# Attention masks of one key tile moved from VectorE to TensorE in a four-layer graph network, with a new written-out order of the work

## The chip, the cores and the metric

The kernel runs on one core of one Trainium2 chip. The metric is the device time of one launch in microseconds (us). TensorE (PE in the profile) multiplies matrices, VectorE (DVE) and ScalarE (ACT) work element by element, GpSimd (POOL) does a few small powers, and SyncE (SP) issues the transfers. The engines run side by side, each through its own list of instructions in order, and wait for each other by semaphores. TensorE writes to PSUM[...].

## The reference, cut to what matters

32 graphs of 512 nodes with 256 features pass through four attention layers; `adj` holds which nodes are neighbours. Layers 0, 1 and 3 are graph attention layers. Layer 2 is a transformer block whose attention has 8 heads of 32 features and is allowed only where either direction of the edge exists, or on the diagonal:

```python
allowed = (adj > 0) | (jnp.swapaxes(adj, 1, 2) > 0) | eye
scores = jnp.einsum('bhqd,bhkd->bhqk', q * scale, k)
scores = jnp.where(allowed[:, None], scores, -jnp.inf)
attn = jax.nn.softmax(scores, axis=-1)
ctx = jnp.einsum('bhqk,bhkd->bhqd', attn, v)
```

After it come an output projection, a layer norm, a feed-forward block of 1024 hidden features, and two more norms. Layers 0 and 1 precede it, layer 3 follows it, and each layer ends in a residual sum and a norm.

## The kernel before, in words

Nodes are cut into R = 4 tiles of P = 128 partitions. One graph of 32 (a batch below) is a Python generator, `graph` (L718), that runs through its stages: loads, layer 0, layer 1, the symmetric mask, qkv, attention, projection, feed forward, layer 3. Each stage is cut by `yield` into units. `paced` (L108) gives each unit a place, `PERIOD * b + PLACES[stage][i]` (L27, L28), and the 32 generators are merged by these places. So the order of the instructions is a list written out by hand, repeated for every batch with a shift of PERIOD; about three and a half batches are in flight at once. The order is fixed as merged for TensorE; the other engines' lists are laid by the framework's scheduler. The size of a place doesn't stand for time on the chip: only the order counts.

What the prediction's steps touch:

- `mask` (L353) makes `at`, the transposed adjacency in bytes, with ScalarE: a cast (L362) and a sum of squares (L370) for each half.
- `symmetric` (L373) makes `a2`: for each half of the rows, VectorE takes the maximum of `at` and a half of `adj` (L381, two rows of tiles in one instruction), then sets the diagonal with a maximum with the identity (L385). `a2` is 0 or 1 in bytes. `adj` and `adjt` halves share one buffer (`half`, L347).
- `qkv` (L483) makes queries and keys. Each is split into a high and a low fp32r part (`hi` on ScalarE L502, `lo` on VectorE L503), and 64 transfers of SyncE (L510) lay four groups of 32 rows out per head, so that one fp32r matmul of 128 rows gives a score at higher precision.
- `attention` (L533): for each of four head pairs and each of four key tiles j, two score matmuls (`s`, 512 columns, one per head) go to PSUM, ScalarE takes the exp (L549), and VectorE multiplies both heads by the mask of that key tile in one instruction of 1024 elements (L550, L551). After the four tiles of a pair come eight context matmuls (`cp`, L557 on), two for each j in the order of j, the two heads in different halves of the columns. `v` holds a column of ones, so the row sums come with them. ScalarE copies the result (`cs`, L567).
- `attended` (L571) turns the contexts by TensorE (`ctp` from `cs`), divides by the row sums on VectorE (L582, L586: `ctx`), turns them again (`ctp` from `ctx`) and projects (`wop`).
- `feed_forward` (L610) alternates `f1p` on TensorE, relu on ScalarE (`ft`, L633) and `f2p`.
- `layernorm` (L259) takes statistics on VectorE (L265, L266, L268), a power of -1/2 on GpSimd (L269), a product on VectorE (L270), and scale and bias on ScalarE (L274). `head_layernorm` (L282), in layer 0, has a power of GpSimd (L296) and then a product on VectorE (L297).
- `along` (L335) spreads a column of exps over all rows by transposes (`gp`) and a copy (`gb`, L344); VectorE makes `pt` from it (L391), and `o` is the product with it.

All matmuls of the program are issued at L101; an fp32 one is two instructions in the profile, an fp32r one and a transpose are one. PSUM is divided into two banks for each of the stages "a" and "c" and four for stage "b", to which qkv, attention and projection belong (`bank`, L247).

In steady state TensorE's list for one batch's length is this (unit and number of the program's matmuls; `ctpv` is `ctp` from `ctx`, `o0` is layer 0's `o`, `o1` layer 1's or 3's; units of several batches lie side by side):

```
s4 f2p4 s2 f1p4 s2 f2p4 cp8 s4 f1p4 s4 f2p4 cp8 xt1p4 f1p4 xt1p4 s4 f2p4
s2 h1p2 f1p4 h1p2 s2 h1p4 f2p4 gp4 cp8 s2 f1p4 s4 f2p4 o1:4 s2 o1:4 cp8
o1:4 ctp4 o1:4 ctp8 h0p2 ctp4 h0p2 ctpv8 xt3p4 h0p4 xt3p4 wop2 h3p2 gp4 h3p6
wop2 gp4 xt2p4 wop2 xt2p4 o0:16 wop2 gp4 o1:4 qkp6 o1:12 o0:16 gp4 ytp4 qkp2
ytp4 vp4 o0:8 f1p4 o0:8 gp4 f2p4 f1p4 o0:8 f2p4 o0:8 f1p4 vp4
```

Of the kernel before, what the change touches and what calls it, by code (L numbers as in the profile page):

```python
# [20 lines left out]


F32R = mybir.dt.float32r


PERIOD = 1205
PLACES = {  # L27
    "edges": [-226, -113, -5, -1],  # L28
    "x": [84],
    "mask": [1464, 1488, 1689, 1689],  # L30
    "layer 0": [
        188, 232, 373, 373, 427, 532, 536, 536, 536, 549, 603, 603, 603, 630, 637, 712, 712, 728,
        758, 758, 766, 779, 787, 791,
    ],
    "layer 1": [1024, 1057, 1078, 1123, 1135, 1135, 1151, 1276, 1299, 1366, 1385],
    "qkv": [1656, 1721, 1771, 1771, 1771, 1849, 1893, 1903, 2016, 2028],
    "attention": [
        1976, 2013, 2122, 2148, 2174, 2174, 2174, 2178, 2178, 2217, 2277, 2277, 2278, 2333, 2363,
        2405, 2452, 2475, 2493, 2527,
    ],  # L40
    "projection": [2590, 2597, 2597, 2606, 2687, 2722, 2820, 2876, 2902, 2949],
    "feed forward": [
        3051, 3062, 3135, 3169, 3169, 3196, 3221, 3327, 3328, 3357, 3381, 3419, 3447, 3483, 3512,
        3560, 3618, 3683,
    ],
    "layer 3": [3958, 3998, 4038, 4074, 4074, 4074, 4082, 4179, 4182, 4185, 4185],
}
STAGES = {"edges": "a", "x": "a", "layer 0": "a", "layer 1": "a", "feed forward": "c", "layer 3": "c"}
ALL = mybir.DependencyInfo(mybir.DependencyClass.Sync, mybir.DependencyReason.DATA)
# [22 lines left out]
def fast_path(ctx: ExitStack, tc: tile.TileContext, a: dict, out: bass.AP, bad: bass.AP):  # L72
# [8 lines left out]
    nc = tc.nc  # L81
    B, N, D = a["x"].shape
    P = 128
    R = N // P
# [15 lines left out]
    def product(what, *args, **kwargs):  # L100
        latest[0] = what(*args, **kwargs).ins.name  # L101

    def in_place(op):

        if latest[0]:
            tc.add_manual_dep(op.ins, latest[0], ALL, reason="in its place")

    def paced(b, name, units):  # L108

        i = 0  # L110
        while True:
            stage[0] = STAGES.get(name, "b")
            try:
# [9 lines left out]
    identb = const.tile([P, P], BF16, name="identb")  # L123
# [115 lines left out]
    sb = ctx.enter_context(tc.tile_pool(name="sb", bufs=1))  # L239
# [107 lines left out]
    def half(b, name, h):  # L347
        t = sb.tile([P, R // 2, N], I32, tag="adj", name=name, bufs=1)
        rows = a[name][b, h * N // 2 : (h + 1) * N // 2]
        nc.sync.dma_start(t, rows.rearrange("(r p) j -> p r j", p=P))  # L350
        return t

    def mask(b):  # L353

        at = sb.tile([P, R, N], U8, tag="at", name="at", bufs=4)
        for h in range(2):
            yield
            t = half(b, "adjt", h)
# [12 lines left out]
        return at  # L371

    def symmetric(b, at):  # L373

        a2 = sb.tile([P, R, N], U8, tag="a2", name="a2", bufs=1)
        for h in range(2):
            yield
            t = half(b, "adj", h)
            rows = slice(h * R // 2, (h + 1) * R // 2)
            yield  # L380
            in_place(nc.vector.tensor_max(a2[:, rows, :], at[:, rows, :], t))  # L381
            for r in range(R // 2):
                own = h * R // 2 + r
                diag = a2[:, own, own * P : (own + 1) * P]
                nc.vector.tensor_max(diag, diag, identb)  # L385
        return a2

    def kept(name, g, edges, f):

# [93 lines left out]
    def qkv(x):  # L483
        xt = yield from transposed([x[:, r, :] for r in range(R)], "xt2")
        qk = []
        for c in range(K):
            t = [sb.tile([P, 2, 2, N], F32R, tag="qk", name="qk", bufs=3) for _ in range(2)]
            for s in range(2):
# [41 lines left out]

        return qk

    def attention(qk, a2):  # L533
        cs = []
        for hp in range(H2 // 2):
            pr = []
            for j in range(R):
                yield
                t = sb.tile([P, 2, N], F32, tag="pr", name="pr", bufs=4)
                for i in range(2):  # L540
                    s = bank("s")
                    product(nc.tensor.matmul,
                    s,
                        qk[hp][:, 1, i, j * P : (j + 1) * P],
                        qk[hp][:, 0, i, :],
                        start=True,
                        stop=True,
                    )
                    nc.scalar.activation(t[:, i, :], s, AF.Exp, scale=QSCALE)  # L549
                edges = a2[:, j, :].unsqueeze(1).to_broadcast([P, 2, N])  # L550
                nc.vector.tensor_mul(t, t, edges)  # L551
                pr.append(t)

            yield
            cp = bank("cp")
            for j in range(R):
                for i in range(2):  # L557
                    first = (2 * hp + i) * VC
                    product(nc.tensor.matmul,
                    cp[i * 2 * DH : (i + 1) * 2 * DH, :],  # L560
                        v[:, j, first : first + 2 * DH],
                        pr[j][:, i, :],
                        start=j == 0,
                        stop=j == R - 1,
                    )
            t = part("cs")
            nc.scalar.copy(t, cp)  # L567
            cs.append(t)
        return cs
# [106 lines left out]
    def load_x(b):  # L676
        xt = sb.tile([P, K, N], F32, tag="xt0", name="xt0", bufs=1)
        nc.sync.dma_start(xt, a["xt"][b].rearrange("(k p) n -> p k n", p=P))
        if b == 0:
            weights0()  # L680
        yield
        x = sb.tile([P, R, D], F32, tag="x", name="x")
        nc.sync.dma_start(x, a["x"][b].rearrange("(r p) d -> p r d", p=P))
        return xt, x

    def layer0_all(b, x, xt, at, rd):
        if b == 0:
# [30 lines left out]
    def graph(b):  # L718
        yield PERIOD * b + PLACES["edges"][0]
        rd = sb.tile([P, ND], F32, tag="rd", name="rd", bufs=3)  # L720
        rds = [rd[:, ends[i] : ends[i + 1]] for i in range(4)]
        if b == 0:
            xt, x = yield from paced(b, "x", load_x(b))
        at = yield from paced(b, "edges", mask(b))
        if b:
            xt, x = yield from paced(b, "x", load_x(b))
        x = yield from paced(b, "layer 0", layer0_all(b, x, xt, at, rds[0]))
        x = yield from paced(b, "layer 1", layer1_all(b, x, at, rds[1]))
        a2 = yield from paced(b, "mask", symmetric(b, at))
        qk = yield from paced(b, "qkv", qkv_all(b, x))  # L730
        cs = yield from paced(b, "attention", attention(qk, a2))
        y = yield from paced(b, "projection", attended_all(b, x, cs, rds[2]))
        x = yield from paced(b, "feed forward", feed_forward_all(b, x, y))
        x = yield from paced(b, "layer 3", layer3_all(b, x, at, rds[3]))
        nc.sync.dma_start(out[b].rearrange("(r p) d -> p r d", p=P), x)
        nc.vector.scalar_tensor_tensor(ok, rd, RD_MIN, ok, op0=ALU.is_ge, op1=ALU.mult)
        nc.vector.scalar_tensor_tensor(ok, rd, RD_MAX, ok, op0=ALU.is_le, op1=ALU.mult)
# [658 lines left out]
```

## Time and profile before

| | |
|---|---|
| runs of the kernel | 3955.46, 3956.56, 3960.7 us; median 3956.56 |
| profiled execution | 3958.95 us, of which the span from first to last instruction is 3957.2 |
| mean granted TensorE clock | 0.973 |
| TensorE, VectorE, ScalarE, GpSimd busy | 3722.2, 2830.4, 1947.7, 362.0 us |
| masking of the probabilities (L551) | 512 instructions, 1216 ns each, 616.7 us busy |
| exp of the scores (L549) | 1024 instructions, 615 ns each |
| scores (`s`) | 1024 matmuls, context (`cp`) 2048 |
| maxima of the mask (L381) | 64 instructions, 1220 ns each |

The profile is of one execution. It gives busy time by engine; the groups of instructions by line; waits, each put down to what ended last; the timeline of each engine; and busy time by windows. In a timeline a line such as "2043.37 2.80 PE L101 MATMUL cp<-pr,v ... x12" says that twelve matmuls that write `cp` from `pr` and `v` began at 2043.37 us and took 2.80 together; what stands in brackets is the time that the engine was idle before, and what ended it. "L101" is the helper's line. The ends of matmuls are modelled and overlap the next one's start, so distances are better taken from start to start.

### The profile page before, as it was taken

How to read it: one execution, taken by the hardware profiler on the slowest of the kernel's cores; microseconds unless marked ns; L12 is line 12 of the kernel's file. 1: busy time of each engine (PE TensorE's matmuls, PEld its weight loads, DVE VectorE, ACT ScalarE, POOL GpSimd, SP SyncE). 2: the span in 40 equal slices, each digit the busy share in tenths (PEclk: the TensorE clock that was granted, in tenths of full speed). 3: DMA queues.
4: the chain of work that ended last, by engine and by line, in shares of the span. 5: the costliest groups of instructions: out<-in, count | busy, mean ns of one | idle time of the engine just before them, and what ended most of it. 6: DMA issues, size and time to landing. Idle time of an engine off the chain costs nothing.

```text
span 3957.2 us, 53344 instructions
## 1 busy us (share of the span) xinstructions
PE 3722.2 (94%) x18982; PEld 2832.6 (72%) x18982; DVE 2830.4 (72%) x5626; ACT 1947.7 (49%) x4257; POOL 362.0 (9%) x266
## 2 busy tenths in 40 slices
PE   5899999999999999999999999999999999999996
PEld 4577777777777777777777777777777777777665
DVE  4667777777777777777777777777777777777753
ACT  2444455544455544455554455544455554555442
POOL 0000010010010101010101010101011101011000
PEclk6899999999999999999999999999999999999998
DMA  3222212222222222222222222222222222221110
GB/s 105 75 72 67 70 58 63 70 75 69 68 58 63 70 75 69 68 61 61 69 75 75 62 64 63 64 75 75 62 64 63 65 79 71 62 67 55 52 50 12
DMA packets 180433, 261.20 MB, mean 66 GB/s; under 512 B 36801, under 2 KB 72769, under 8 KB 180161
## 3 DMA queue, kind: packets, MB, share of 16 engines
q1 hardware_dynamic: 180160, 257.71, 23.0%
q8 instruction: 154, 2.52, 0.3%
q14 instruction: 119, 0.97, 0.1%
HBM read 106.57 MB, written 16.78 MB: 31 GB/s over the span
## 4 chain that ended last, share of the span: by engine, by line
PE 51%; DVE 17%; issue 10%; ACT 7%; POOL 7%; SPq 2%; DMA 1%; DVEq 0%; POOLq 0%; ACTq 0%
PE o L101 12%; PE f1p L101 7%; PE f2p L101 6%; DVE pr L551 5%; PE cp L101 4%; POOL rs L269 4%; PE qkp L101 3%; PE h3p L101 3%; POOL st L296 3%; PE wop L101 3%; PE h1p L101 3%; ACT y L274 2%; SPq L510 2%; DVE bn L265 2%; ACT pr L549 2%
## 5 line engine op out<-in xcount | busy, mean ns | idle before, releaser
L551 DVE TENSOR_TENSOR pr<-pr,a 128x1024 f32<-128x1024 f32 x512 | 616.7, 1216 | 220.4 <-ACT pr L549 220.2
L391 DVE SCALAR_TENSOR_TENSOR pt<-gb,ex,at 128x512 f32<-128x512 f32 x768 | 533.3, 743 | 136.3 <-ACT gb L344 136.3
L274 ACT ACTIVATE y<-y,rs 128x256 f32<-128x256 f32 x768 | 397.9, 589 | 386.0 <-DVE rs L270 385.9
L549 ACT ACTIVATE pr<-s 128x512 f32<-128x512 f32 x1024 | 542.3, 615 | 68.7 <-PE s L101 68.3
L101 PE MATMUL cp<-pr,v 128*64 128x512 f32 x2048 | 485.0, 605 | 64.7 <-DVE pr L551 64.7
L101 PEld LDWEIGHTS o<-hv,pt 128*128 128x128 f32 x4096 | 506.1, 198 | 32.6 <-DVE pt L391 16.0
L101 PE MATMUL o<-hv,pt 128*128 128x65 f32 x4096 | 507.2, 280 | 15.4 <-DVE pt L391 11.3
L101 PE MATMUL f2p<-wf,ft 128*128 128x256 f32 x2048 | 492.5, 383 | 23.2 <-ACT ft L633 22.9
L101 PE MATMUL f1p<-yt,wf 128*128 128x256 f32 x2048 | 488.7, 381 | 0.3 <-DVE yt L301 0.3
L101 PE MATMUL o<-h,pt 128*128 128x257 f32 x2048 | 482.5, 383 | 3.2 <-DVE pt L391 3.1
L101 PEld LDWEIGHTS o<-h,pt 128*128 128x128 f32 x2048 | 381.1, 190 | 97.0 <-ACT y L274 23.5
L101 PEld LDWEIGHTS f2p<-wf,ft 128*128 128x128 f32 x2048 | 379.1, 190 | 95.6 <-ACT ft L633 46.8
L633 ACT ACTIVATE ft<-f1p,cols 128x256 f32<-128x256 f32 x512 | 216.7, 479 | 454.5 <-PE f1p L101 454.5
L269 POOL TENSOR_TENSOR rs<-rs,mhalf 128x4 f32<-128x4 f32 x192 | 234.9, 1224 | 2146.4 <-DVE rs L268 2092.5
L101 PEld LDWEIGHTS f1p<-yt,wf 128*128 128x128 f32 x2048 | 382.4, 190 | 52.3 <-issue 0.8
L101 PEld LDWEIGHTS cp<-pr,v 128*64 128x64 f32 x2048 | 127.9, 137 | 346.0 <-DVE pr L551 150.3
L101 PE MATMUL s<-qk 128*128 128x512 f32 x1024 | 359.1, 456 | 1.8 <-ACT pr L549 1.7
L265 DVE BATCH_NORM_STATS2 bn<-y 128x6 f32<-128x256 f32 x768 | 295.8, 409 | 3.5
L101 PEld LDWEIGHTS s<-qk 128*128 128x128 f32 x1024 | 187.0, 190 | 97.9 <-issue 52.7
L101 PE MATMUL qkp<-xt,wqkv 128*128 128x512 f32 x512 | 232.2, 596 | 0.9 <-DVE xt L301 0.9
L296 POOL TENSOR_TENSOR st<-st,mhalf 128x16 f32<-128x16 f32 x32 | 120.9, 3779 | 978.3 <-DVE st L295 978.3
L567 ACT COPY cs<-cp 128x512 f32<-128x512 f32 x128 | 74.5, 582 | 259.6 <-PE cp L101 259.6
(129 smaller groups left out, 4500.0 us busy)
## 6 DMA issues: line engine op xcount, KB each, us to landing
qk<-hi SPq DMA_DIRECT2D x1024, 64.0 KB, 2.0
qk<-lo SPq DMA_DIRECT2D x1024, 64.0 KB, 2.0
adjt<-in_adjt SPq DMA_DIRECT2D x64, 512.0 KB, 3.3
adj<-in_adj SPq DMA_DIRECT2D x64, 512.0 KB, 3.4
xt<-in_xt SPq DMA_DIRECT2D x32, 512.0 KB, 3.6
x<-in_x SPq DMA_DIRECT2D x32, 512.0 KB, 3.6
out<-y SPq DMA_DIRECT2D x32, 512.0 KB, 3.1
wf<-in_w1t SPq DMA_DIRECT2D x1, 1024.0 KB, 7.9
```

Source lines behind the costliest of these rows:

```text
L101: latest[0] = what(*args, **kwargs).ins.name
L265: nc.vector.bn_stats(st[:, r, :], y[:, r, :])
L269: nc.gpsimd.tensor_tensor(rs[:, 1, :], rs[:, 0, :], mhalf[:, :R], op=ALU.pow)
L274: nc.scalar.activation(y[:, r, :], y[:, r, :], AF.Identity, bias=rs[:, 2, r : r + 1], scale=rs[:, 1, r : r + 1],)
L296: nc.gpsimd.tensor_tensor(st[:, 2, :], st[:, 1, :], mhalf[:, :G], op=ALU.pow)
L391: nc.vector.scalar_tensor_tensor(t, g, f, edges, op0=ALU.max, op1=ALU.mult)
L510: nc.sync.dma_start(t[hh // 2][g * DH : (g + 1) * DH, s, hh % 2, :].bitcast(F32), src[hh * DH : (hh + 1) * DH].bitcast(F32),)
L549: nc.scalar.activation(t[:, i, :], s, AF.Exp, scale=QSCALE)
L551: nc.vector.tensor_mul(t, t, edges)
L567: nc.scalar.copy(t, cp)
L633: nc.scalar.activation(ft[:, f, :], p[:, f, :], AF.Relu, bias=bf1[:, ff + f : ff + f + 1])
```

## The change

1. `symmetric` makes masks of tiles 0 to 2 as before, in bytes, but one row of tiles in each instruction. That of tile 3 goes into a bf16 tile `shut`, which is then turned into 0 where an edge is allowed and -2^127 where not, by one more instruction of VectorE.
2. In `attention`, for j = 3 each score gets a second matmul into the same bank, identity times `shut`, both bf16, which adds the mask to the score before the exp; the multiplication on VectorE is left out for that tile. For j = 0 to 2 nothing changes.
3. PERIOD and all of PLACES are new, in units of a tenth of the old ones.

```diff
+SHUT = -(2.0**127)
-PERIOD = 1205
+PERIOD = 12054
 PLACES = {
...
     "attention": [
-        1976, 2013, 2122, 2148, 2174, 2174, 2174, 2178, 2178, 2217, 2277, 2277, 2278, 2333, 2363,
-        2405, 2452, 2475, 2493, 2527,
+        20262, 20932, 21922, 21982, 22092, 22092, 22092, 22350, 22350, 23077, 23537, 23537,
+        24028, 24208, 24328, 24532, 25064, 25220, 25368, 25943,
     ],
...
     def symmetric(b, at):
 
-        a2 = sb.tile([P, R, N], U8, tag="a2", name="a2", bufs=1)
+        a2 = sb.tile([P, R - 1, N], U8, tag="a2", name="a2", bufs=1)
+        shut = sb.tile([P, N], BF16, tag="shut", name="shut", bufs=1)
+        parts = [a2[:, r, :] for r in range(R - 1)] + [shut]
         for h in range(2):
             yield
             t = half(b, "adj", h)
-            rows = slice(h * R // 2, (h + 1) * R // 2)
             yield
-            in_place(nc.vector.tensor_max(a2[:, rows, :], at[:, rows, :], t))
-            for r in range(R // 2):
-                own = h * R // 2 + r
-                diag = a2[:, own, own * P : (own + 1) * P]
+            for r in range(h * R // 2, (h + 1) * R // 2):
+                in_place(nc.vector.tensor_max(parts[r], at[:, r, :], t[:, r % (R // 2), :]))
+                diag = parts[r][:, r * P : (r + 1) * P]
                 nc.vector.tensor_max(diag, diag, identb)
-        return a2
+        nc.vector.tensor_scalar(shut, shut, 0.0, SHUT, op0=ALU.is_equal, op1=ALU.mult)
+        return a2, shut
...
                         start=True,
-                        stop=True,
+                        stop=j < R - 1,
                     )
+                    if j == R - 1:
+                        product(nc.tensor.matmul, s, identb, shut, start=False, stop=True)
                     nc.scalar.activation(t[:, i, :], s, AF.Exp, scale=QSCALE)
-                edges = a2[:, j, :].unsqueeze(1).to_broadcast([P, 2, N])
-                nc.vector.tensor_mul(t, t, edges)
+                if j < R - 1:
+                    edges = a2[:, j, :].unsqueeze(1).to_broadcast([P, 2, N])
+                    nc.vector.tensor_mul(t, t, edges)
```

With it TensorE's list for one batch's length becomes (`s*` is a score of j = 3 followed by its identity product; all else as above):

```
s4 f2p4 s2 f1p4 s*2 f2p4 cp8 s4 f1p4 s2 s*2 f2p4 f1p4 cp8 xt1p8 f2p4
h1p2 s4 f1p4 h1p6 s2 f2p4 gp4 s*2 cp8 s2 f1p4 s4 f2p4 o1:4 s*2 o1:4 cp8
o1:4 ctp16 o1:4 h0p2 xt3p8 ctpv4 h0p2 ctpv4 h0p4 wop2 h3p2 wop2 h3p2 gp4 wop2 h3p4
gp4 xt2p8 wop2 o0:16 gp4 o1:8 qkp6 o1:8 o0:16 gp4 ytp4 qkp2
ytp4 vp4 o0:12 f1p4 o0:4 gp4 f2p4 f1p4 o0:8 f2p4 o0:8 f1p4 vp4
```

SyncE has the same transfers in both; in the new order the two loads of `adj` no longer follow each other, the load of `xt` stands between them. On VectorE the third mask of the first head pair now stands ahead of the step that feeds GpSimd's power (L295); before, it stood between that step and the product that waits for the power (L297), and the mask of j = 3 stood behind the product. On ScalarE a pair of mask instructions (L362, L370) stands ahead of the copy `cs` of the fourth head pair.

More of the change, by code (lines that the diff above doesn't have):

```diff
@@ L23 @@
 F32R = mybir.dt.float32r
-PERIOD = 1205
+SHUT = -(2.0**127)
+PERIOD = 12054
 PLACES = {
-    "edges": [-226, -113, -5, -1],
-    "x": [84],
-    "mask": [1464, 1488, 1689, 1689],
+    "edges": [-1440, -1440, -410, 1420],
+    "x": [3260],
+    "mask": [16220, 16520, 16600, 17520],
     "layer 0": [
-        188, 232, 373, 373, 427, 532, 536, 536, 536, 549, 603, 603, 603, 630, 637, 712, 712, 728,
-        758, 758, 766, 779, 787, 791,
-    ],
-    "layer 1": [1024, 1057, 1078, 1123, 1135, 1135, 1151, 1276, 1299, 1366, 1385],
-    "qkv": [1656, 1721, 1771, 1771, 1771, 1849, 1893, 1903, 2016, 2028],
+        2410, 3594, 4534, 4534, 5073, 5753, 5753, 5823, 6123, 6123, 6233, 6233, 6603, 6773, 6903,
+        7687, 7687, 7777, 8077, 8077, 8157, 8287, 8439, 8439,
+    ],
+    "layer 1": [11037, 11066, 11277, 11729, 11849, 11879, 12043, 13286, 13554, 14195, 14884],
+    "qkv": [17180, 17740, 18270, 18270, 18270, 18990, 19484, 19654, 21635, 21635],
     "attention": [
-        1976, 2013, 2122, 2148, 2174, 2174, 2174, 2178, 2178, 2217, 2277, 2277, 2278, 2333, 2363,
-        2405, 2452, 2475, 2493, 2527,
+        20262, 20932, 21922, 21982, 22092, 22092, 22092, 22350, 22350, 23077, 23537, 23537,
+        24028, 24208, 24328, 24532, 25064, 25220, 25368, 25943,
     ],
-    "projection": [2590, 2597, 2597, 2606, 2687, 2722, 2820, 2876, 2902, 2949],
+    "projection": [26801, 26801, 26861, 26911, 27661, 27721, 28721, 29140, 29256, 29848],
     "feed forward": [
-        3051, 3062, 3135, 3169, 3169, 3196, 3221, 3327, 3328, 3357, 3381, 3419, 3447, 3483, 3512,
-        3560, 3618, 3683,
+        31013, 31120, 32042, 32263, 32263, 32465, 32710, 33771, 33983, 34076, 34284, 34691,
+        35070, 35329, 35615, 36103, 36646, 37299,
     ],
-    "layer 3": [3958, 3998, 4038, 4074, 4074, 4074, 4082, 4179, 4182, 4185, 4185],
+    "layer 3": [39714, 39714, 40906, 41226, 41406, 41526, 41526, 42359, 42359, 42379, 42379],
 }
@@ L531, in qkv, with attention @@
         return qk
-    def attention(qk, a2):
+    def attention(qk, a2, shut):
         cs = []
@@ L730, in graph @@
         qk = yield from paced(b, "qkv", qkv_all(b, x))
-        cs = yield from paced(b, "attention", attention(qk, a2))
+        cs = yield from paced(b, "attention", attention(qk, *a2))
         y = yield from paced(b, "projection", attended_all(b, x, cs, rds[2]))
```

## Prediction

> **What bounds the kernel now.** I read the page's first two parts first.
>
> ```profile
> PE 3722.2 (94%) x18982; PEld 2832.6 (72%) x18982; DVE 2830.4 (72%) x5626; ACT 1947.7 (49%) x4257; POOL 362.0 (9%) x266
> ...
> PEclk6899999999999999999999999999999999999998
> ```
>
> TensorE (PE) is busy 94%; nothing else is close. The time is therefore TensorE's work plus what TensorE waits. Waits by waiting engine, TensorE's own, show who keeps it (us in total, times, longest):
>
> ```profile
> PE cp L101 <- DVE pr L551: 64.7, 65, 1.9
> PE ctp L101 <- DVE ctx L586: 51.3, 61, 1.7
> PE f2p L101 <- ACT ft L633: 22.9, 39, 3.2
> ```
>
> 65 waits in 32 batches is two a batch for masked probabilities, and two for the contexts. Ends of matmuls are modelled, so these totals are too small; I take stalls from start to start in the timeline of TensorE (start, us, ..., number of instructions; one fp32 matmul of the program is two).
>
> ```profile
> 1967.61 3.65 PE L101 MATMUL cp<-pr,v 128*64 128x512 f32 x16
> 1971.19 2.00 PE L101 MATMUL o<-h,pt 128*128 128x257 f32 x8
> ...
> 2040.13 0.82 PE L101 MATMUL s<-qk 128*128 128x512 f32 x2
> 2041.44 1.99 PE L101 MATMUL f2p<-wf,ft 128*128 128x256 f32 x8 [0.49 <-ACT ft L633]
> 2043.37 2.80 PE L101 MATMUL cp<-pr,v 128*64 128x512 f32 x12
> 2047.01 1.08 PE L101 MATMUL cp<-pr,v 128*64 128x512 f32 x4 [0.84 <-DVE pr L551]
> 2048.01 1.28 PE L101 MATMUL s<-qk 128*128 128x512 f32 x4
> ...
> 2053.60 2.79 PE L101 MATMUL cp<-pr,v 128*64 128x512 f32 x12
> 2057.51 1.08 PE L101 MATMUL cp<-pr,v 128*64 128x512 f32 x4 [1.11 <-DVE pr L551]
> 2058.52 0.65 PE L101 MATMUL xt1p<-ident,y 128*128 128x128 f32 x4
> ```
>
> An unhindered context group takes 3.58 us (1967.61 to 1971.19). The first head pair's takes 4.64, the second's 4.92: stalls of 1.06 and 1.34, each in front of the last four matmuls, key tile j=3. Pairs three and four have none. The feed-forward product behind the first pair's last scores starts 1.31 after those began, where the pair before them was followed after 0.66 (2037.94 to 2038.60): 0.65 lost. VectorE's timeline tells why the first mask is late: it stands behind a normalization that waits for GpSimd.
>
> ```profile
> 2044.59 1.22 DVE L297 TENSOR_TENSOR y<-y,st 128x1024 f32<-128x1024 f32 x1 [2.79 <-POOL st L296]
> 2045.73 1.22 DVE L551 TENSOR_TENSOR pr<-pr,a 128x1024 f32<-128x1024 f32 x1
> ```
>
> The third stall, once a batch, in TensorE's timeline, and then in the busy time by windows (length; busy PE, PEld, DVE, ACT, POOL; clock; DMA):
>
> ```profile
> 2095.60 0.38 PE L101 MATMUL ctp<-ident,ctx 128*128 128x128 f32 x2
> 2096.24 0.33 PE L101 MATMUL ctp<-ident,ctx 128*128 128x128 f32 x1 [0.26 <-DVE ctx L586]
> 2098.01 1.16 PE L101 MATMUL ctp<-ident,ctx 128*128 128x128 f32 x5 [1.44 <-DVE ctx L586]
> ```
>
> ```profile
> 2095.00:2098.20 3.20, 1.50 (x9) 0.92 (x8) 3.15 (x12) 2.61 (x6) 0.00 (x0) 1.00 0.00 0
> 2098.20:2102.00 3.80, 3.80 (x15) 3.35 (x15) 2.34 (x6) 2.52 (x5) 1.01 (x1) 0.55 0.28 105
> ```
>
> Eight transposes take 0.87; in another batch they run from 1978.39 to 1981.40, so 2.14 is stall. After it the clock falls to about half in many batches: on the chain the GpSimd powers of L296 follow each other by 118.9 us (7 of 10 batches) or 117.2 (3), 118.43 on average. The halved clock costs 1.2 a batch.
>
> [...] No bf16 matmul is in this trace; the nearest row is the one-pass fp32r score, also 512 columns. Eight f1p and four scores take 2.65 (2049.13 to 2051.78); less 8 x 0.216 this leaves 0.23 a score[...]. [...] here fp32 loads of 190 hide under 216 to 230. [...] Here 1.50 busy of 3.20 was enough[...]: a half-idle window may do it. [...]
>
> **The change, part by part**, per batch in steady state. Orders are from both kernels' instruction lists, which hold no times.
>
> *Identity products.* Eight bf16 matmuls of 512 columns on TensorE, the bound. Each 0.23 (the score's step[...]): +1.84. [...] High end: if the load of ident doesn't hide, 0.23 + 0.19 = 0.42, +3.4. [...]
>
> *Masks that go.* Four L551 a batch, 4 x 1.22 = 4.9 on VectorE; the two maxima of 1.22 become four of 0.69, and one small bf16 tensor_scalar, some 0.3, is added: VectorE net -4.2. It isn't the bound, so this is worth only the stalls. Tile j=3 now needs scores and exp alone, which end 2.6 or more before its context matmuls want them (three pairs of tiles run first). First pair: stall gone, -1.06; its j=0 to 2 masks stand ahead of the GpSimd wait, as before. Second pair: -1.34 for j=3. But the third mask now stands ahead of L295 (GpSimd starts 1.2 later), a `lo` of 0.74 stands in the same chain, and the bo addition (1.2) ahead of the second pair's j=2; against this the j=3 mask (1.2) behind the normalization is gone. So VectorE is 1.4 to 2 later there while TensorE is about 1 earlier; an f1p group (1.73) moved ahead of the contexts covers most. I count it from row durations: j=2 is masked 0.5 after it is wanted: +0.5.
>
> *Feed-forward product.* The two identity products put 0.46 of cover between f1p and f2p: 0.65 becomes 0.2, -0.45.
>
> *Contexts.* All sixteen head transposes now stand together, then o (1.73), h0p (0.9), xt3p x8 (0.87), and only then the context transposes. VectorE needs four times 0.6: covered, -2.14, and -1.2 for the clock if no half-idle window is left. What is late next is xt3p, ahead of them, which wants layer 2's second norm. In the kernel before that was ready (L274, 1978.06 + 2.07) 16.55 after the last f2p (1963.58). In the new order TensorE arrives after about 14.8. The j=3 mask (1.2) is gone from the chain and the context steps stand behind it, L476 and L478 (1.3) ahead: 15.65, so +0.65. ScalarE's mask casts L362 and L370 (2.3) now stand before the copy `cs` of the fourth pair: about 0.3 late for the transposes, +0.3.
>
> *Layer 3.* The transposes for gb3 now follow h3p directly; before, wop x4 (0.87) stood between and hid the h copy (0.37), the exp (0.21) and two handovers. With that cover gone, +0.85.
>
> *Layer 0.* A third of o's four rows moves ahead of f1p, and `lo` leaves the run of pt products: the stall of 0.32 there (sixteen o from 2017.20 to 2019.28, 2.08 against 16 x 0.11) goes, -0.3.
>
> *SyncE.* The same loads; the second adj half now stands behind the xt load, which waits for h0p. It lands 3.4 us after issue and its maximum is over 8 us later: nothing; if that cover fails, the maximum and, behind it on VectorE, xt2 wait for it. Sixty-four qk copies keep their places.
>
> Sum: 1.84 + 0.5 + 0.65 + 0.3 + 0.85 - 1.06 - 1.34 - 0.45 - 2.14 - 1.2 - 0.3 = -2.35 a batch. Thirty batches run in this state (start and drain left as they are): -70. The profiled execution took 3958.95 (span 3957.2 and 1.75 around), 2.4 above the median of the runs: 3888.5 from it, 3886 from the median. I take 3887.
>
> **The rivals.**
> - *The new waits are smaller than counted.* VectorE has 28% idle and is relieved. If half of the 2.3 of new waits don't come: -3.5 a batch, 3852. For it: my counts leave no credit for waits that overlap. Against: each hangs on a named chain.
> - *The change doesn't do what it says: the stalls only move.* The norm before xt3p ends as late as now; TensorE waits there, and the clock halves as now. Then the 2.14 + 1.2 and the +0.95 against them cancel: -2.35 + 2.39 = about 0, 3958. For it: the chain before was 16.55 long, 1.8 longer than the new order allows.
> - *Slower: the change of type.* Each bf16 product stands between fp32r scores. If the loads on both sides are exposed (0.19 each, the score's own load), a product costs 0.61, not 0.23: +3.0 a batch, net +0.7, 3977. It decides from 0.23 + 2.35/8 = 0.52. Against: fp32 and fp32r follow each other now without such a cost.
>
> **How the numbers follow.** A measurement of this kernel can tell about 0.2% (8 us) from no change. Chances: the count (3866 to 3915) 0.48; smaller waits (3838 to 3866) 0.18; stalls moved, wholly or partly (3915 to 3962) 0.19, of which 0.06 is within 0.2%; type change or a like cost, slower, 0.13; faster still 0.02. Faster 0.48 + 0.18 + 0.13 + 0.02 = 0.81, same 0.06, slower 0.13. The range, 3838 to 3960, leaves out the last two and the edge of the third; it holds the high end of the products (0.19 x 8 x 30 = +46: 3933).
>
> **What would show it.** Right: no wait of cp on pr, small waits of xt3p on L274's successor and of gp on ex3, PEclk at 1.00 after the contexts, starts of score and identity product 0.23 apart, 116 us between successive powers. Wrong: identity products over 0.5 apart, or a wait of 2 us at xt3p with the clock halved behind it.

## The result, and the profile after

The changed kernel takes 3909.1 us (median of four runs, 3906.41 to 3910.59) against 3957.5 for the kernel before in the same session: a ratio of 0.9876, 95% interval 0.9862 to 0.989. The profiled execution has a span of 3904.6 us and a mean granted TensorE clock of 0.983 (before: 0.973). The gain is 48.4 us or 1.61 us a batch over thirty batches, where 70 were forecast.

GpSimd's power in layer 0's norm marks the batches. Before, its starts were 118.9 or 117.2 us apart, 118.4 on average. After (L297; line numbers of the changed kernel are one to five higher), from GpSimd's timeline:

```profile
1898.55 2.90 POOL L297 TENSOR_TENSOR st<-st,mhalf 128x16 f32<-128x16 f32 x1 [29.83 <-DVE st L296]
2015.33 2.90 POOL L297 TENSOR_TENSOR st<-st,mhalf 128x16 f32<-128x16 f32 x1 [29.83 <-DVE st L296]
```

They are 116.77 or 116.78 apart all through the steady state: 1.63 less a batch, and thirty times that is 49 us, the whole gain. The page's first part:

```profile
PE 3753.3 (96%) x19238; PEld 2824.5 (72%) x19238; DVE 2674.8 (69%) x5594; ACT 1926.2 (49%) x4257; POOL 346.9 (9%) x266
```

TensorE is busier than before (3722.2), VectorE less busy (2830.4). A mask on VectorE (L556) costs what it did, 1216 ns; there are 384 instead of 512. The maxima of 512 elements (L384), which the forecast put at 0.69 us, take 0.675 into bytes and 0.684 into `shut` (rows of 512 elements took 0.683 at L647 and 0.687 at L478 before), and the new instruction that scales `shut` (L387) takes 0.283. TensorE's waits after (us in total, times, longest):

```profile
PE xt3p L102 <- ACT y L275: 31.1, 94, 12.0
PE gp L102 <- ACT ex L665: 22.9, 32, 1.0
...
PE cp L102 <- DVE pr L556: 17.1, 30, 2.7
```

Before, `cp` on `pr` had 64.7 us and `ctp` on `ctx` 51.3. The second is gone and the first is a quarter. Two new ones have come: `gp` had 0.7, and `xt3p` 16.9 in two waits, where it now waits 94 times. In one batch of TensorE's timeline: the identity products, the contexts of the second head pair, and the two new waits.

```profile
1896.87 0.58 PE L102 MATMUL s<-qk 128*128 128x512 f32 x1
1897.30 0.39 PE L102 MATMUL s<-shut,identb 128*128 128x512 bf16 x1
...
1897.98 1.95 PE L102 MATMUL f2p<-wf,ft 128*128 128x256 f32 x8
...
1911.24 1.94 PE L102 MATMUL cp<-pr,v 128*64 128x512 f32 x8
1913.66 1.94 PE L102 MATMUL cp<-pr,v 128*64 128x512 f32 x8 [0.49 <-DVE pr L556]
1915.53 1.10 PE L102 MATMUL xt1p<-ident,y 128*128 128x128 f32 x8
...
1950.07 1.05 PE L102 MATMUL h0p<-w,xt 128*128 128x264 f32 x4
1951.12 0.33 PE L102 MATMUL xt3p<-ident,y 128*128 128x128 f32 x1
1951.61 0.33 PE L102 MATMUL xt3p<-ident,y 128*128 128x128 f32 x1 [0.16 <-ACT y L275]
...
1953.20 0.60 PE L102 MATMUL ctp<-ident,ctx 128*128 128x128 f32 x4
...
1961.56 2.01 PE L102 MATMUL h3p<-w3g,xt 128*128 128x258 f32 x8
1964.27 0.65 PE L102 MATMUL gp<-ident,ex 128*128 128x128 f32 x4 [0.70 <-ACT ex L665]
```

Two scores with their products take 1.11 (1896.87 to 1897.98); two plain scores take 0.66, so a product is 0.225. Only such sums can be read: a score's start and its product's lie 0.43 apart, the product's and the next score's 0.03, and a score with its product takes 0.46 (1896.87 to 1897.33). The sixteen `cp` of the second pair take 4.29 where 3.58 is their pace: 0.71 of stall, each end read from the next start. From the `h0p` ahead of `xt3p` to the `ctp` behind it are 3.13 us; four `h0p` take 0.89 (1953.64 to 1954.53 elsewhere) and eight transposes 0.87, so 1.37 is stall. That is more than the brackets show (0.16 each at 1951.61, 1952.10 and 1952.60), since they are counted from modelled ends. `h3p` to `gp` is 2.71 for eight products of 1.74 in all: 0.97. And the clock, busy time by windows behind that stretch (length; busy PE, PEld, DVE, ACT, POOL; clock; DMA):

```profile
1953.60:1958.00 4.40, 4.40 (x24) 3.83 (x23) 4.33 (x11) 2.38 (x7) 0.55 (x1) 1.00 0.02 6
```

The window ahead, 1949.00 to 1953.60, has TensorE 4.11 of 4.60 us busy, with the wait in short pieces; the clock granted behind it is 1.00, where in the stretch that the prediction shows it was 0.55. Over the 27 batches from the third power of layer 0 to the thirtieth, the trace's record of the granted clock has 18 spells of half clock before, of 3.41 us each, and one after, in the first of these batches. The clock in a spell is 0.5 in that record; from these numbers I estimate that a spell loses half of its length and that the spells before cost 1.1 a batch (1.2 in the forecast).

### The profile page after: what moved, and what is told of

Read it like the earlier page. It is cut to its first block, busy times and chain, and to the rows that moved or that the text cites. A ratio compares the mean times of both kernels' runs of the same rounds, so it can differ in the third digit from the quotient of the medians.

```text
span 3904.6 us, 53602 instructions
## 1 busy us (share of the span) xinstructions
PE 3753.3 (96%) x19238; PEld 2824.5 (72%) x19238; DVE 2674.8 (69%) x5594; ACT 1926.2 (49%) x4257; POOL 346.9 (9%) x266
## 3 DMA queue, kind: packets, MB, share of 16 engines
q1 hardware_dynamic: 180160, 257.71, 23.1%
## 4 chain that ended last, share of the span: by engine, by line
PE 60%; DVE 14%; issue 8%; ACT 5%; POOL 5%; POOLq 0%; ACTq 0%
PE o L102 16%; PE f1p L102 7%; PE f2p L102 6%; PE qkp L102 5%; PE cp L102 5%; DVE pr L556 4%; ACT y L275 4%; POOL rs L270 3%; PE h3p L102 3%; PE s L102 3%; PE h1p L102 3%; PE wop L102 3%; POOL st L297 2%; PE gp L102 2%; PE vp L102 2%
## 5 line engine op out<-in xcount | busy, mean ns | idle before, releaser
L556 DVE TENSOR_TENSOR pr<-pr,a 128x1024 f32<-128x1024 f32 x384 | 459.1, 1216 | 319.3 <-ACT pr L553 319.2
L102 PE MATMUL f2p<-wf,ft 128*128 128x256 f32 x2048 | 491.6, 383 | 12.3 <-ACT ft L638 12.2
L102 PE MATMUL cp<-pr,v 128*64 128x512 f32 x2048 | 474.9, 600 | 17.8 <-DVE pr L556 17.1
L270 POOL TENSOR_TENSOR rs<-rs,mhalf 128x4 f32<-128x4 f32 x192 | 246.2, 1282 | 2118.8 <-DVE rs L269 1826.0
L102 PEld LDWEIGHTS f2p<-wf,ft 128*128 128x128 f32 x2048 | 380.1, 191 | 69.5 <-ACT ft L638 17.1
L102 PE MATMUL s<-qk 128*128 128x512 f32 x1024 | 395.1, 481 | 1.6 <-ACT pr L553 1.6
L345 ACT COPY gb<-gp 128x512 f32<-128x512 f32 x192 | 111.5, 581 | 219.4 <-PE gp L102 219.4
L428 DVE RECIPROCAL rd<-o 128x4 f32<-128x4 f32 x128 | 23.4, 183 | 272.7 <-PE o L102 272.7
```

The costliest lines, as they stand in the source:

```text
L270: nc.gpsimd.tensor_tensor(rs[:, 1, :], rs[:, 0, :], mhalf[:, :R], op=ALU.pow)
L345: nc.scalar.copy(g, p)
L428: nc.vector.reciprocal(rdh, o[:, :, HO:])
```

## The experiments

The theory after the result: the forecast's mechanism holds, the masks' stalls and the contexts' stall go, and the shortfall is new waits (`xt3p`, `gp`, second pair) that were priced too low. Rivals: the new order alone does it; the identity products alone do it; the products cost more or less than 0.225; the new waits can be won back by moving two steps.

### The two halves apart

**e1: the kernel before with PERIOD and PLACES of the changed one, all masks on VectorE.**

```diff
-PERIOD = 1205
+PERIOD = 12054
 PLACES = {
...
```

> The new order with all four masks on VectorE. Theory A (the gain comes from the first two head pairs' waits that the identity products take away, and from the order of the contexts; the two need each other): TensorE saves the eight products (8 x 0.225 = 1.8 us a batch), but the mask of j = 3 comes late again in pairs one, two and three (about 1.1, 1.5 and 0.5 a batch) and f2p waits 0.45 more; net some +1.5 a batch, about 3950 us, with waits of cp on pr back at 60 us or more. Theory B (the order alone brings the gain): 3909 less 30 x 1.8, about 3855 us, cp waits below 30 us.

Measured: 3951.05 us, ratio to before 0.9979 (0.9971 to 0.9987), powers 118.2 apart: theory A's time. Its waits of TensorE:

```profile
PE cp L101 <- DVE pr L551: 79.0, 66, 3.1
PE xt3p L101 <- ACT y L274: 36.2, 93, 12.1
```

The order alone takes the contexts' stall away (no row of `ctp` on `ctx` is left) and raises the mean granted clock to 0.982 (0.973 before, 0.983 in the changed kernel), and it brings `xt3p` and `gp` (23.1); what is left of its gain is 8.5 us. The stall on `pr` it makes no smaller, 79.0 against 64.7. So of the changed kernel's waits those of `xt3p` and `gp` belong to the order, and what the identity products give is `cp`'s: 17.1 in place of 79.0.

**e2: the changed kernel with PERIOD and PLACES of the one before.**

```diff
-PERIOD = 12054
+PERIOD = 1205
 PLACES = {
...
```

> The identity products in the old order. Theory A: the waits of cp go (-2.4 us a batch), f2p's halves (-0.45), the products cost 1.8, and the stall at the contexts stays for the most part (about 1.7 of 2.14, the clock halved behind it in part of the batches): about -1.5 a batch, 3905 to 3915 us. The new waits on layer 2's second norm and on gb3 do not appear. Theory B: without the new order no gain, 3950 us or more.

Measured: 4004.84 us, ratio 1.0113 (1.0096 to 1.013). Theory A failed; the time is in theory B's range.

```profile
PE h0p L102 <- ACT exp L477: 57.1, 30, 1.9
```

The stalls at `pr` are gone as expected (8.5 us left), and the stall of the contexts with them (5.4). In their place `h0p` waits for its bank until ScalarE's exp of layer 1 has read it, 1.9 us a batch, and `h3p` for its input (32.6). ScalarE's timeline, of the kernel before and then of e2, tells why that exp is late:

```profile
1976.88 0.47 ACT L475 ACTIVATE exp<-o,rd 128x256 f32<-128x256 f32 x1
1978.06 2.07 ACT L274 ACTIVATE y<-y,rs 128x256 f32<-128x256 f32 x4 [0.71 <-DVE rs L270]
```

```profile
2001.32 2.07 ACT L275 ACTIVATE y<-y,rs 128x256 f32<-128x256 f32 x4 [0.73 <-DVE rs L271]
...
2003.65 0.45 ACT L477 ACTIVATE exp<-o,rd 128x256 f32<-128x256 f32 x1
```

Layer 1's last exp stood ahead of layer 2's norm and stands behind it in e2. `h3p`'s input comes from a copy on VectorE that now stands behind the sum of L400 (2009.55, the copy 2010.68) and stood ahead of it (1985.17 and 1984.26). TensorE's order is that of before; the framework has laid the lists of the two other engines anew, as in e3 and e4 below. So e2 changes more than the masks, and what the identity products would be worth in the old order with those lists as they were stays open. As measured, neither half is worth the whole: -8.5 us for the order, +45 for the masks, -48 for both.

### The price of the identity products

**e3: each identity product twice, with half the constant, so that the sum is the same.**

```diff
-SHUT = -(2.0**127)
+SHUT = -(2.0**126)
...
+                        product(nc.tensor.matmul, s, identb, shut, start=False, stop=False)
                         product(nc.tensor.matmul, s, identb, shut, start=False, stop=True)
```

> As the changed kernel, with each identity product made twice and the mask halved (2^126), so that the sum is the same. It measures the price of one product on the path: at 0.225 us each 8 x 0.225 = 1.8 a batch, of which the waits at xt3p and before the second pair's contexts may take in up to 0.8: 1.0 to 1.8 a batch, 3939 to 3963 us. If a product between two types cost 0.4 or more, 4005 us or more.

Measured: 4109.62 us, ratio 1.038 (1.0363 to 1.0397). 256 products of 0.225 are 58 us; this is 200 more than the changed kernel takes, in the range that I had given to a dear product. One wait tells where it is from, and it isn't the products': `f2p` on `ft` (L639) has 114.3 us, 38 times, up to 3.8, where the changed kernel has 12.2. The scheduler that lays ScalarE's list had put layer 0's norm ahead of the two relus that `f2p` wants. So the price can't be read here; e11 and e12 below do it.

**e11: without the identity products of head pairs one and two. e12: without all of them.** Nothing takes their place: the fourth key tile is left unmasked there, so part of the computation is missing.

```diff
-                        stop=j < R - 1,
+                        stop=j < R - 1 or hp < 2,
...
-                    if j == R - 1:
+                    if j == R - 1 and hp > 1:
```

> The changed kernel without the identity products of the first two pairs of heads; nothing takes their place, so there the fourth key tile is left without its mask (that part of the computation is left out). The lists of ScalarE and VectorE are those of the changed kernel but for two instructions, so the products' price can be read: 128 of them at 0.225 us are 28.8 us of TensorE. If TensorE's time is what counts where they stand, 3880-3886 us. If they lie where TensorE waits anyway (pair two's wait for pr, 0.7 us a batch, grows by what they leave), 3885-3900 us. If a change of type inside an accumulation costs 0.6 us instead of 0.23 beyond what the trace shows, 3830-3845 us.

> The same with all 256 identity products left out, the fourth tile unmasked in all pairs (left out). 57.6 us of TensorE at 0.225 us each. If all of it is on the path, 3850-3856 us; if xt3p and gp, whose steps on ScalarE don't come earlier, take back part of it as longer waits, 3856-3885 us; no change of the time if the products were covered.

Measured: e11 3903.63 us (ratio 0.9867, 0.9852 to 0.9883), e12 3884.91 us (0.9816, 0.9803 to 0.9829). e11 lies above all three ranges of its expectation, e12 at the upper end of its second. Of 28.8 us of TensorE in pairs one and two 5.5 come out, less than the 6 us by which the interval reaches to either side; in the steady state nothing does, the powers are 116.8 apart in both. The time comes back as waits: in e11 `cp` on `pr` has 28.7 us (17.1 in the changed kernel) and `f2p` on `ft` comes 38 times (11). From start to start, `f2p` follows the first pair's last two scores after 1.07 (1894.61 to 1895.68; 1.11 with the products), and the second pair's sixteen `cp` take 4.77 (1908.50 to 1913.27; 4.29). So 0.41 and 0.48 of the four products' 0.90 come back there. VectorE's timeline tells what sets that: the reciprocal behind layer 0's last sums, and the third mask of the second pair. In the changed kernel, and then in e11:

```profile
1888.64 0.18 DVE L428 RECIPROCAL rd<-o 128x4 f32<-128x4 f32 x1 [5.34 <-PE o L102]
...
1912.39 1.22 DVE L556 TENSOR_TENSOR pr<-pr,a 128x1024 f32<-128x1024 f32 x1
```

```profile
1886.38 0.18 DVE L428 RECIPROCAL rd<-o 128x4 f32<-128x4 f32 x1 [5.34 <-PE o L102]
...
1910.13 1.22 DVE L556 TENSOR_TENSOR pr<-pr,a 128x1024 f32<-128x1024 f32 x1
```

23.75 us in both. From layer 0's sums to the second pair's contexts it is VectorE's list, with its two waits for GpSimd, that sets the time, and TensorE's four products lie beside it. Those of pairs three and four are on the path for the most part: from e11 to e12 18.7 of 28.8 us come out (the powers of e12 are 116.2 apart), while `ctp` on `cs` takes back 12 (14.8 us against 2.7). VectorE's list is the same in e11 as in the changed kernel, and ScalarE's but for one cast of the mask (L363, ahead of layer 0's norm instead of behind it); in e12 a few more steps have changed places. All in all the products cost 24.2 us of the 55 that the forecast put on them. A dear change of type is ruled out by the trace: 0.61 a product would be 1.22 for two, and two scores with both products take 1.11.

**e7: identity products in pairs one and two alone; pairs three and four multiply on VectorE again,** by `shut` compared with 0.

```diff
+                elif not (hp < 2):
+                    edges = shut.unsqueeze(1).to_broadcast([P, 2, N])
+                    nc.vector.scalar_tensor_tensor(
+                        t, edges, 0.0, t, op0=ALU.is_equal, op1=ALU.mult
+                    )
```

> The changed kernel with the identity products in the first two pairs of heads alone; pairs three and four multiply their fourth tile on VectorE again, from the same bfloat16 tile. TensorE loses 120 products of 0.225 us, 27 us. If all of the gain comes from the first two pairs (where the stalls on pr were), 3880-3890 us. If VectorE's time in pairs three and four is what made the normalised contexts late before (51.3 us of ctp waiting for ctx, with the halved clock behind them), that wait comes back: 3915-3965 us with ctp's wait at 25-55 us.

Measured: 3943.76 us, ratio 0.9961 (0.9947 to 0.9975): 34.7 slower than the changed kernel. That is the size which the rival gave, but the wait is at another place:

```profile
PE cp L102 <- DVE pr L559: 44.4, 33, 1.8
```

TensorE waits 1.39 us a batch in the third pair, for the mask that came back (L559); no wait for `ctx` has come. TensorE is spared 27 us of products and waits 44.4 at `cp`, 4.9 more at `xt3p` and 8.6 more at `ctp` on `cs`: 31 of the 34.7. In the old order the third pair had no stall on `pr`; in the new one it has (e1's are 0.98 in the first pair and 1.39 in the third). So in this order the third pair needs the products too. The fourth shows no stall in e7; it wasn't tried alone.

### The new waits

**e4: layer 3's fourth `gp` behind `xt2p`,** so that its exp is ready.

```diff
-    "layer 3": [39714, 39714, 40906, 41226, 41406, 41526, 41526, 42359, 42359, 42379, 42379],
+    "layer 3": [39714, 39714, 40906, 41226, 41406, 41526, 41850, 42359, 42359, 42379, 42379],
```

> As the changed kernel, with the transposes for layer 3's gb3 moved behind xt2p (one place changed). Theory A: their wait on the exp (0.95 us a batch) is covered by 0.87 of transposes: -0.9 a batch, about 3882 us. Rival: the products that use gb3 become late instead, and the time stays at 3909 us.

Measured: 4086.29 us, ratio 1.0321 (1.0304 to 1.0339): 177 us slower than the changed kernel, for one step of 0.43 us moved; neither theory had that. The wait of `gp` is gone (1.4 us left), and `f2p` waits 121.9 us for `ft`. TensorE's timeline, then ScalarE's:

```profile
1995.11 1.92 PE L102 MATMUL f2p<-wf,ft 128*128 128x256 f32 x4 [3.79 <-ACT ft L638]
```

```profile
1989.11 0.48 ACT L638 ACTIVATE ft<-f1p,cols 128x256 f32<-128x256 f32 x1 [0.34 <-PE f1p L102]
1992.61 2.08 ACT L275 ACTIVATE y<-y,rs 128x256 f32<-128x256 f32 x4 [3.02 <-DVE rs L271]
1994.60 0.46 ACT L638 ACTIVATE ft<-f1p,cols 128x256 f32<-128x256 f32 x1
```

Layer 0's norm, which waits 3.02 us for its statistics, stands between the two relus of one unit. In the changed kernel it stands behind them. PLACES fixes TensorE's list alone. ScalarE's is laid anew by the framework, and with the step that was moved on TensorE another has moved there that takes nothing from it. The eight `f1p` behind it (1996.82 to 1999.58) take 2.76 where eight take 1.73 in the changed kernel (1919.98 to 1921.71), and the four `f2p` ahead of them 1.71, where eight take 1.82 (1980.66 to 1982.48): the clock granted from 1995.11 to 1999.58 was 0.62. 3.79 of stall and, by these two groups, an estimated 1.8 of clock are most of the 6 us by which a batch is longer (122.8).

**e5: e4 with only that norm put behind,** by a `yield` ahead of it with a late place; TensorE's order is e4's.

```diff
-        7687, 7687, 7777, 8077, 8077, 8157, 8287, 8439, 8439,
+        7687, 7687, 7777, 8077, 8077, 8157, 8287, 8439, 8439, 10300,
...
         nc.vector.tensor_add(y, y, x)
+        yield
         layernorm(y, 1e-5)
```

> The same TensorE order as e4, layer 3's fourth gb transposes late as there; only the instructions of layer 0's norm are put to the lists later, so that on ScalarE they stand behind the two relus between which they stood in e4. If what cost e4 its 177 us was that one relu behind a waiting norm (3.8 us of f2p waiting for ft in most batches, and the halved clock behind it), f2p's wait for ft falls from 122 us to about 12 and the time to 3885-3925 us. If it was the later gb itself (its pt late for layer 3's sums, 35 us of o waiting for pt, and what follows), the time stays at 4050-4090 us.

Measured: 3913.84 us, ratio 0.9891 (0.9876 to 0.9906). 172 of the 177 us are gone, and ScalarE's list differs from e4's in that norm alone: it was the relu behind the norm. What the later `gp` itself does is seen now:

```profile
PE o L102 <- DVE pt L393: 36.1, 42, 2.3
```

`gp` on `ex` falls from 22.9 us to 1.4, `o` on `pt` grows from 13.4 to 36.1: the wait has only moved on.

**e8: `xt3p` behind the first context transposes and a group of `h0p`. e6: that, and `gp` behind the last `wop`.**

```diff
-    "layer 3": [39714, 39714, 40906, 41226, 41406, 41526, 41526, 42359, 42359, 42379, 42379],
+    "layer 3": [39757, 39757, 40906, 41226, 41406, 41526, 41526, 42359, 42359, 42379, 42379],
```

(e8's diff; e6 has 41903 for the second 41526 as well.)

> One of e6's two moves alone: xt3p later. If the wait of xt3p on y is a matter of some 1 us of place, its 31.1 us fall to 5-15 us and the time to 3885-3895 us (e6 then gains the gb part, some 22-28 us, on top). If ScalarE's y is late for all that follows too, the wait moves to h0p or ctp and the time stays at 3905-3912 us.

> The changed kernel with two of TensorE's steps later by some instructions: the transposes xt3p behind the first context transposes and a group of h0p, and layer 3's fourth gb behind the last projection products. Both waits of the changed kernel that were priced too low or missing are meant to lose their cause: xt3p on ScalarE's y (31.1 us) should fall to 10 us or less and gp on ex (22.9 us) to 2 us or less. If these waits are what stands between forecast and result, 3865-3885 us. Rival: they only move (o waits for pt as in e4, or h0p for the y behind it), 3900-3930 us.

Measured: e8 3923.36 us (ratio 0.9914, 0.9901 to 0.9928), e6 4057.71 us (1.0254, 1.024 to 1.0268). Both expectations that I favoured failed, and both times lie above their rivals' ranges too. In e8's timeline of TensorE:

```profile
1961.34 0.66 PE L102 MATMUL ctp<-ident,ctx 128*128 128x128 f32 x2 [0.24 <-DVE ctx L591]
1962.92 1.16 PE L102 MATMUL h0p<-w,xt 128*128 128x264 f32 x4 [0.93 <-ACT exp L477]
1963.92 1.04 PE L102 MATMUL xt3p<-ident,y 128*128 128x128 f32 x8
```

`xt3p` waits no more, but what stood behind it does: the transposes for `ctx`, then `h0p` for the bank that ScalarE's exp still reads. From the first `h0p` to the first `wop` it is 7.33 us (1959.68 to 1967.01), in the changed kernel 6.68 (1950.07 to 1956.75). The 1.3 us at `xt3p` were the cover of both. In e6, `o` waits for `pt` 83.5 us in all, and batches of 120.0 and 122.6 us follow each other. The mean granted clock is 0.967, in the changed kernel 0.983; in one batch ten `o` take 4.45 us (1922.85 to 1927.30) where sixteen take 3.48 (1932.99 to 1936.47). What sets the lower clock off I didn't follow further.

**e9: e5's `gp`, without its `yield`, and four of the query-key products ahead of layer 3's sums, which gives `pt` 1.8 us. e10: e9 with `xt3p` behind the first `ctp` group alone.**

```diff
-    "qkv": [17180, 17740, 18270, 18270, 18270, 18990, 19484, 19654, 21635, 21635],
+    "qkv": [17180, 17740, 18250, 18270, 18270, 18990, 19484, 19654, 21635, 21635],
...
-    "layer 3": [39714, 39714, 40906, 41226, 41406, 41526, 41526, 42359, 42359, 42379, 42379],
+    "layer 3": [39716, 39716, 40906, 41226, 41406, 41526, 41850, 42359, 42359, 42379, 42379],
```

(The diff is e10's; e9 leaves 39714 as it was.)

> The changed kernel with layer 3's fourth gb behind xt2p, as in e4 and e5, and the first four query-key projection products (1.8 us) put ahead of layer 3's first sums, so that these give pt the time which it lacked in e5 (0.73 us a batch). On ScalarE layer 0's norm stands between no two relus. If waits of this size are settled by their own neighbours alone, gp's 22.9 us and o's 36 us both go: 3878-3892 us. If each step made later only moves the wait to the next one, 3905-3920 us.

> e9 with xt3p behind the first group of context transposes (not behind h0p too, as in e8). xt3p's wait of 1.3 us a batch covers part of what the transposes would wait for ctx, by e8 some 0.9 us of two groups: if 0.5 us a batch can be had here, 10-15 us below e9; if the wait only changes its name, within 5 us of e9.

Measured: e9 3898.59 us (ratio 0.985, 0.9836 to 0.9863), e10 3895.3 us (0.9842, 0.9828 to 0.9855). Both beat the changed kernel, by some 10 and 14 us (powers 116.4 and 116.3 apart). e9 lies between the two ranges of its expectation; e10's 3 us on e9 is within what its expectation called a change of name. In e9 21.5 us of `gp`'s wait are gone, and 17.2 have come back at `o`: on `pt` 19.2 (13.4 in the changed kernel), and a new one on `y` of 11.4. The wait of the second pair (17.1) is down to 2.8.

## Why the forecast held, and which terms were mis-sized

The forecast was faster, 3887 us in a range of 3838 to 3960; the measured 3909.1 lies 22 us above it and within. The case that came is "the count". Of its signs, the small waits of `xt3p` and `gp`, the clock of 1.00 behind the contexts and powers near 116 us apart were there. `cp` still waits for `pr` in the second pair (17.1 us), and the 0.23 between a score and its product can be read from sums alone. Per batch, in us:

| step of the prediction | counted | measured after |
|---|---|---|
| identity products, time of TensorE | +1.84 | 8 x 0.225 = +1.80 |
| first pair's stall | -1.06 | -1.06 (`cp` x16 in 3.58) |
| second pair: stall gone, new one for the third mask | -1.34 + 0.5 | -1.34 + 0.71 |
| feed-forward product | -0.45 | -0.65 |
| contexts' stall, halved clock | -2.14 - 1.2 | both gone, taken as -2.14 - 1.2 |
| `xt3p` on the second norm | +0.65 | +1.37 |
| `ctp` on the late `cs` | +0.3 | +0.15 (sixteen in 1.89) |
| `gp` behind `h3p` | +0.85 | +0.97 |
| layer 0's `o` | -0.3 | gone, taken as -0.3 |
| sum | -2.35 | -1.69; by the powers -1.63 |

**The term that fell short is `xt3p`.** The prediction let layer 2's second norm end 15.65 after the last `f2p` ends, and TensorE arrive after about 14.8. That is 0.85 apart, and its +0.65 doesn't say where the other 0.2 go; in the trace after, too, the stall is 0.22 less than the two times are apart (1.37 of 1.59), as long as two of the eight transposes. Counted in the same way in the trace after (from 1936.51), the norm's last row is done at 1952.55, which is 16.04, and TensorE could begin at 1950.96, which is 14.45: the first `h0p` and its 0.89. Both errors go the same way, 0.39 and 0.35. The first is in the list of VectorE: two steps of layer 1 (L478 and L480, 0.66 and 0.68) now run among the norm's statistics, while only one `ctx` of 0.39 left that place; I had let about 1.0 leave. The second is the wait for `cs`, counted at 0.3 ahead of it and seen at 0.15, and the rest small sums. `xt3p` gives 0.72 of the shortfall, the second pair 0.21, `gp` 0.12, and the other terms give 0.39 back, which makes the 0.66 between the two sums. The 0.06 by which the powers differ from the sum I can't assign.

**"Contexts: -2.14" was right in the sum but not by itself.** e8 shows that `ctx` isn't ready when the transposes could begin; `xt3p`'s wait stands ahead and covers it. The two terms are one: 2.14 of stall became 1.37, and the clock stayed at 1.00 (1953.60 to 1958.00). Why it did wasn't tested.

**"TensorE, the bound", at +1.84, was right as time of TensorE, not as a price.** By e11 and e12 the four products of the first two pairs cost nothing a batch, and all eight 24 us in place of 55. The sum came out nearly right because the waits for the first pair's `f2p` and the second pair's `cp` were counted with the products in place: in e11, without them, these are longer by what the products took. TensorE at 96% busy isn't the bound in every stretch; from layer 0's sums to the second pair's contexts VectorE and GpSimd are (23.75 us with the products and without).

**The rivals.** "Smaller waits" falls: they were larger. "The stalls only move" is true to a third (`xt3p` and `gp` take 2.3 of the 6.7 a batch that went; e1 shows that they come with the order), but the clock did not halve (1.00 behind the contexts). "The change of type" is ruled out by the 0.225 of a product. Not thought of at all was that the gain hangs on both parts: e1 is 8 us faster than before, and e2, with its other lists, 45 slower.

**What was taken for safe and is not:** the lists of ScalarE and VectorE. The prediction read them for the kernel at hand; what it took wrongly from VectorE's is the part of the `xt3p` chain above. But e3 and e4 changed nothing on ScalarE and lost 177 to 200 us there, and e5 shows for e4 that one norm's position did it (for e3 and e2, seen in their timelines, it wasn't tested).

## What to carry to other kernels

Leave out the work that a busy engine does, and see what the time does, before you price it at its duration: 28.8 us of matmuls at an engine that is 96% busy gave back 5.5 us here, where another engine's chain ran beside them (e11). A wait that is taken away uncovers those behind it, so count what is late next, and from both sides: when the awaited step ends and when the engine now arrives. Where only one engine's order is written down, compare all engines' lists after each move, for a waiting instruction that has come between two that others need.

## What the runs showed of the hardware

**A power of GpSimd took 0.91 us longer where a mask of VectorE had begun ahead of it.** The power of layer 0's norm (L296 before, L297 after) took 3.81 us before and 2.90 after, on the same tile, in every batch whose power starts between 400 and 3400 us (25 before, 26 after). Before, a mask ran on VectorE when it began; after, VectorE waits for the power and does nothing. VectorE's timeline of the kernel before (the power ran from 1923.55 to 1927.36) and of the changed one (from 1898.55 to 1901.45):

```profile
1923.37 1.22 DVE L551 TENSOR_TENSOR pr<-pr,a 128x1024 f32<-128x1024 f32 x1
```

```profile
1901.48 1.23 DVE L298 TENSOR_TENSOR y<-y,st 128x1024 f32<-128x1024 f32 x1 [3.01 <-POOL st L297]
```

The overlap with the mask was 1.04 us, the power 0.91 longer. The small power of four columns shows the same: 1.01 with VectorE waiting (1968.52, before), 1.99 when an addition of 1.19 had begun 0.07 ahead of it (1910.29, after). The powers end 2.77 behind the mask's end and 0.87 behind the addition's, a little less than the 2.90 and 1.01 that they take with VectorE waiting. But where a maximum of VectorE begins 0.06 behind a small power, neither is longer than elsewhere (1.01, and 1.22 where the mean is 1.220). GpSimd's and VectorE's timelines, before:

```profile
1981.11 1.01 POOL L269 TENSOR_TENSOR rs<-rs,mhalf 128x4 f32<-128x4 f32 x1 [3.35 <-DVE rs L268]
```

```profile
1981.17 1.22 DVE L381 TENSOR_TENSOR a<-at,adj 128x1024 uint8<-128x1024 uint8 x1
```

In the first two cases a VectorE instruction had begun ahead of the power, by 0.18 and 0.07 us; the third shows that an overlap alone doesn't lengthen it. What lengthens it wasn't tested. The prediction left this out; it took the third mask ahead of the power as a pure delay of 1.2, of which the shorter power gives 0.9 back.

**The clock.** Behind one wait of 3.79 us (e4) the granted clock was 0.62 for 4.47 us, and the eight `f1p` there took 2.76 from start to start where 1.73 is usual (2024.96 to 2026.69 before the change). Before the change, it was 0.55 for 3.80 us behind the prediction's stretch of 1.50 busy of 3.20. The batch ahead of that one has the same stall of 2.14 (1978.39 to 1981.40) and keeps a clock of 1.00 (length; busy PE, PEld, DVE, ACT, POOL; clock; DMA):

```profile
1978.40:1981.40 3.00, 1.30 (x9) 0.87 (x8) 2.83 (x11) 2.50 (x7) 0.29 (x1) 1.00 0.00 0
1981.40:1985.20 3.80, 3.80 (x24) 3.36 (x23) 2.79 (x7) 3.48 (x9) 0.72 (x1) 1.00 0.43 141
```

So the length of a stall doesn't decide alone: behind waits of 0.26 and 1.44 us at the contexts the clock was 0.55 in one batch, and behind 0.26 and 1.45 in the one ahead of it 1.00. What else decides stays open. Behind waits of 1.37 in all within 3.1 us (after) it was 1.00.

**A bf16 product between fp32r scores took 0.225 us.** One more fp32r score of the same 512 columns took as much (four take 1.11, 1918.87 to 1919.98; two 0.66, 1924.14 to 1924.80); no cost of the change of type shows in these sums.
